# Image loads on ScalarE's queue, and small set-up steps moved between engines, in a two-layer table convolution

## The chip, the core and the metric

The kernel runs on one core of a Trainium2 chip. A core has four engines that compute: TensorE (matrix products, "PE" in the profile, with its weight loads as "PEld"), VectorE ("DVE"), ScalarE ("ACT") and GpSimd ("POOL"). Each works through its own list of instructions in order and waits for the others by semaphores. SyncE ("SP") only begins transfers here. Transfers between the chip's memory (DRAM) and the core's on-chip memory (SBUF) are done by 16 DMA engines; TensorE writes into a small memory of its own (PSUM), which VectorE and ScalarE read. The metric is the device time of one execution in microseconds (us), the lower the better.

## What is computed

The input x holds 16 images of 256 channels, 28 x 28. It is normalised in groups of 8 channels (`_gn`), and goes through two convolutions that are computed by tables: each channel's 3 x 3 patch is compared with 16 centroids, a softmax over the 16 turns the distances into weights, and the weights pick from a table that holds each centroid's product with the convolution's weights.

```python
def amm_conv3x3(x, centroids, w_sub, stride=1):
    ...
    d = jnp.sum(p * p, axis=-1)[..., None] - 2.0 * jnp.einsum('bncs,cks->bnck', p, centroids) + jnp.sum(centroids * centroids, axis=-1)[None, None]
    attn = jax.nn.softmax(-d, axis=-1)
    lut = jnp.einsum('cks,cso->cko', centroids, w_sub)
    out = jnp.einsum('bnck,cko->bno', attn, lut)
...
out = amm_conv3x3(x, centroids1, wsub1, stride=1)
out = jax.nn.relu(bn_inference(out, bn1_gamma, bn1_beta, bn1_mean, bn1_var))
out = amm_conv3x3(out, centroids2, wsub2, stride=1)
out = bn_inference(out, bn2_gamma, bn2_beta, bn2_mean, bn2_var)
out = se_layer(out, se_w1, se_b1, se_w2, se_b2)
return jax.nn.relu(out + x)
...
x = x + _L0_conv_ref(_gn(x), ...)
```

`bn_inference` scales and shifts each channel with given statistics; `se_layer` scales each channel by a gate worked out from the channels' means.

## The kernel before

**Blocks and steps.** The first layer is done for all 16 images, then the second. An image is cut into four blocks: two halves of 128 channels (hh) by two halves of 14 rows (t), 392 positions each, in the order (0,0), (0,1), (1,1), (1,0). A block takes two steps, an image eight; step 8b is the first of image b in the first layer.

**A block's work.** For a block the 3 x 3 patches lie in two buffers, `pts[0]` and `pts[1]`, one for each half of the 128 channels' groups. The products of patches and centroids, the logits (`logits`, L609), are computed by 32 x 32 tiles in four groups, each into two PSUM banks of a pair; ScalarE takes their exponentials (`exps`, L620). With these, `num_b` (L674, "nb") gives the sums of the softmax's denominators, which are taken apart by `split_r` (L684) and `split_q` (L694) on ScalarE and `join_r` (L688) and `join_q` (L699) on VectorE and inverted by `recip_dve` (L702); `spread` (L713, L717) copies the inverses across partitions. `num_a` (L660, "na") sums the weights of the 16 centroids into nine codes; they are scaled by the inverses either by VectorE straight from PSUM (`scale_a`, L736) or copied by ScalarE (`copy_a`, L730) and scaled by GpSimd (`scale_q`, L725). Then come the table products with 128 x 128 tiles (`product`, L744), for which GpSimd first makes differences of two blocks' codes (`mix`, L753): by a scheme like Strassen's, an image's 2 x 2 blocks need seven products in place of eight. `acc_copy`, `acc_add`, `reg_add` and `norm_out` put the results together.

**Order.** The order is written out by hand. `at(step, sub, f, ...)` files a job under a pair of numbers; at the end all jobs are run through in the order of the pairs, and each puts its instructions at the end of its engine's list. Two jobs with different pairs stand in that order on every engine that both use, and in every DMA queue. PSUM is handed out in four tags of two banks each (0 to 3, "bank" and "banks" in the code); for the first image a table gives the tags. A job that writes a bank waits until the one before has been read.

**Images.** Images of the first layer are loaded whole (`load_x`, L186, into `xt`), normalised (`gn_stats`, `gn_mean` L530, `gn_var`, `gn_apply`) and written into a padded copy in DRAM, `home`; a block's patches are read from there by six transfers (`patches`, at step g + p - 2, sub 1.5, p = 0 or 1), all begun by SP. `load_x(b + 1)` stands at step 8b - 2, sub 2.6, and so behind a step's six patch transfers in SP's queue. In the second layer `load_x` brings the image for the last sum.

**The first image.** No patches of a normalised image exist yet at the start. So the first image's patches are taken from the raw x, loaded straight into `pts` and into `alts` (the buffers of the table, "wall" in the profile, which are filled with 1.0 first, since patches at the rim have places that no transfer writes), and the normalisation is put into the centroids: each centroid weight is scaled by the group's inverse deviation, and shifted in such a way that the mean falls out. The steps for one half of the channels, each once for either half h of the nine taps' weights:

- `raw_stats`, `raw_mean`, `raw_dev`, `raw_root`: statistics of the groups, up to a power of -0.5 on GpSimd (L473), the "root";
- `sq_act`, `sq_sum` (L374), `sq_add`: the sum of squares of the centroids;
- `mean_off`: subtracts the mean over the 16 centroids from the weights (a reduction and an add);
- `raw_scales`: spreads the root to 16 columns (L477, VectorE), brings them by a product with `eighth` (L478, "gnq") to all partitions and makes from it the scales `scm` (L481) and shifts `ms`;
- `tap_sum` (L390): a product that sums the weights of a tap, `tap_scale` (L397): weights times scale, `tap_shift` (L405 multiplies the tap's sum by the shift into `tmp`, L408 adds it);
- `border` (L512, L515, and GpSimd's L512, L520, L525): adds the mean's terms at the rim of the patches.

```python
def tap_shift(hh, h):
    tmp = rpool.tile([P, N], F32, tag="r", name="tmp")[:, :256].rearrange("p (g n) -> p g n", n=32)
    ...
    nc.vector.tensor_tensor(
        tmp, raws.pop(("tap", hh, h)).rearrange("p (g n) -> p g n", n=32), of16(raws["ms", hh], h), ALU.mult
    )
    nc.vector.tensor_tensor(w, w, tmp, ALU.add)
```

These steps come for channel half 0 before the first logits (the steps of h = 1 partly between them), and for channel half 1 within the first steps (`later`, step 1, sub 0.9; `later_tap` and `tap_shift` at step 3). ScalarE fills `alts[1]` and GpSimd `alts[0]` (L1487). `setup_bn` (step 6, sub 2.75) makes the scales and shifts of both layers' `norm_out`: four steps on GpSimd (L311, L312) and VectorE's small steps behind them (L326 among them), in one function. Image 1 is normalised within step 4: `gn_mean` at 0.81, `gn_var` at 0.83, `acc_copy` at 0.85, the shuffles that `scale_a` of block 1 needs at 0.815 and 0.835.

A flag that is summed at the end decides whether a loop behind the main program computes everything a second time in a safer way; for these inputs it is not entered.

## Time and profile before

| | |
|---|---|
| median of 3 runs | 2611.18 us (2610.99 to 2613.4) |
| the profiled execution, its own time | 2614.36 us |
| its span in the trace | 2612.9 us |
| TensorE's products (PE) / weight loads (PEld) | 99% / 49% of the span |
| VectorE / ScalarE / GpSimd | 68% / 52% / 73% |
| the DMA queue that SP and ScalarE use | 48% of 16 engines' span |
| read from DRAM / written | 288.46 MB / 77.95 MB |

How to read the rows below. A row of groups or waits names the engine, the operation, the tile written and the tiles read ("out<-in") and the line of the kernel; a row of the timeline begins with the start and the duration in us from the start of the span, then the engine, the line and the shape, "xN" instructions taken together, and in brackets the idle time of the engine just before with the work that ended it ("issue" where the profile shows none). A row of waits ends in the sum of the waits in us, their number, and the longest. A row of stretches gives the stretch, its length, then the busy time of TensorE, weight loads, VectorE, ScalarE and GpSimd with the number of instructions, the granted clock of TensorE, the DMA engines' busy share, and GB/s. "SPq" is the start of a transfer from SP's queue.

### The profile page before, as it was taken

Reading aid. Unit: us, or ns where it says so; the run is one execution under the profiler, and the core shown is the slowest. Engines: PE = TensorE matmul, PEld = TensorE weight load, DVE = VectorE, ACT = ScalarE, POOL = GpSimd, SP = SyncE. Lnnn points to the kernel's source line nnn. Section 1 sums busy time; section 2 is a strip of 40 time slices with the busy share of each in tenths; the row PEclk is TensorE's granted clock in tenths of the full one; section 3 lists DMA queues with packets and bytes.
Section 4 is the critical chain, followed back from the end, with each engine's and each line's share of the span. In section 5 each row is a group of like instructions: output and inputs, shape, how many; then the busy total and the mean of one; then the engine's idle time right before and its main releaser. Section 6 shows DMA issues by size and latency. Waiting matters only on the chain.

```text
span 2612.9 us, 85829 instructions
## 1 busy us (share of the span) xinstructions
PE 2590.2 (99%) x37026; PEld 1273.7 (49%) x37026; DVE 1779.5 (68%) x3798; ACT 1369.3 (52%) x1912; POOL 1908.8 (73%) x1341
## 2 busy tenths in 40 slices
PE   8999999999999999999999999999999999999998
PEld 3444454444444444444444444444444444444444
DVE  8776656666566665566666776767776667767676
ACT  5444444444444454444454655555555655555565
POOL 6786666866568766676666787778878788787786
PEclk9999999999999999999999999999999999999999
DMA  6556656665555566655664444444444444444442
GB/s 212 152 150 183 201 155 186 165 170 165 159 143 144 170 182 179 170 154 141 176 172 107 106 118 119 126 115 117 104 130 123 120 117 110 115 126 127 117 104 66
DMA packets 213288, 372.07 MB, mean 142 GB/s; under 512 B 29496, under 2 KB 183528, under 8 KB 212328
## 3 DMA queue, kind: packets, MB, share of 16 engines
q1 hardware_dynamic: 206584, 333.75, 48.0%
q0 software_dynamic: 6176, 32.66, 3.5%
q8 instruction: 295, 4.83, 0.8%
q14 instruction: 89, 0.73, 0.1%
q10 hardware_dynamic: 144, 0.10, 0.0%
HBM read 288.46 MB, written 77.95 MB: 140 GB/s over the span
## 4 chain that ended last, share of the span: by engine, by line
PE 97%; DVE 1%; POOL 1%; issue 0%; ACT 0%; DMA 0%; SPq 0%; ACTq 0%; POOLq 0%
PE acc L744 52%; PE lg L609 17%; PE nb L674 14%; PE na L660 14%; POOL qp L753 0%; DVE rb L717 0%; DVE r L702 0%; PE sep L1045 0%; ACT e L620 0%; PE sep L1037 0%; DMA xt<-in_x 0%; DVE gn_st L424 0%; DVE qp L736 0%; DVE first L477 0%; PE tap L390 0%
## 5 line engine op out<-in xcount | busy, mean ns | idle before, releaser
L744 PE MATMUL acc<-qp,wall 128*128 128x392 f32 (+1 forms) x3088 | 1097.7, 498 | 0.3 <-POOL qp L753 0.2
L620 ACT ACTIVATE e<-lg 128x784 f32<-128x784 f32 x960 | 738.2, 820 | 642.9 <-PE lg L609 639.7
L753 POOL TENSOR_TENSOR qp<-qp,qp 128x784 f32<-128x784 f32 x512 | 945.0, 1870 | 153.3 <-DVE qp L736 152.9
L744 PEld LDWEIGHTS acc<-qp,wall 128*128 128x128 f32 x3088 | 568.5, 190 | 503.9 <-issue 53.0
L717 DVE STREAM_SHUFFLE rb<-r 128x392 f32<-128x392 f32 x1024 | 551.1, 605 | 0.0
L609 PE MATMUL lg<-pt,wd 32*32 32x392 f32 x15872 | 470.1, 499 | 1.0 <-DMA pt<-home 0.4
L688 DVE SCALAR_TENSOR_TENSOR r<-nb,kst,r 128x392 f32<-128x392 f32 x128 | 80.0, 625 | 445.1 <-ACT r L684 444.4
L674 PE MATMUL nb<-e,cwb 64*32 64x392 f32 x8192 | 374.1, 492 | 0.4 <-ACT e L620 0.3
L660 PE MATMUL na<-e,cwa 64*32 64x392 f32 x8192 | 374.3, 492 | 0.0
L736 DVE TENSOR_TENSOR qp<-na,rb 128x784 f32<-128x784 f32 x352 | 333.7, 972 | 59.1 <-PE na L660 47.3
L725 POOL TENSOR_TENSOR qo<-qo,rb 128x392 f32<-128x392 f32 x128 | 131.3, 1026 | 299.3 <-DVE rb L713 298.6
L702 DVE RECIPROCAL r<-r 128x392 f32<-128x392 f32 x128 | 333.2, 2603 | 4.4
L725 POOL TENSOR_TENSOR qp<-qp,rb 128x784 f32<-128x784 f32 x160 | 295.9, 1860 | 3.0
L674 PEld LDWEIGHTS nb<-e,cwb 64*32 64x32 f32 x8192 | 190.9, 107 | 174.2 <-issue 23.8
L660 PEld LDWEIGHTS na<-e,cwa 64*32 64x32 f32 x8192 | 183.0, 106 | 182.2 <-issue 73.8
L609 PEld LDWEIGHTS lg<-pt,wd 32*32 32x32 f32 x15872 | 116.7, 103 | 268.4 <-issue 241.0
L744 PE MATMUL acc<-qp,w_A 128*128 128x392 f32 x512 | 182.7, 499 | 0.0
L684 ACT ACTIVATE r<-nb,kst 128x392 f32<-128x392 f32 x128 | 86.7, 677 | 166.4 <-PE nb L674 163.3
L644 POOL TENSOR_TENSOR z<-z,mx 128x1568 f32<-128x1568 f32 x32 | 91.8, 2869 | 94.8 <-DVE mx L638 94.8
L744 PE MATMUL acc<-qo,wall 128*128 128x392 f32 (+1 forms) x386 | 157.9, 491 | 0.0
L730 ACT COPY qp<-na 128x784 f32<-128x784 f32 x160 | 130.0, 813 | 22.0 <-PE na L660 20.5
L744 PEld LDWEIGHTS acc<-qp,w_A 128*128 128x128 f32 x512 | 94.7, 190 | 82.1 <-DVE qp L736 19.8
(242 smaller groups left out, 1713.3 us busy)
## 6 DMA issues: line engine op xcount, KB each, us to landing
pt<-home SPq DMA_DIRECT2D x744, 209.0 KB
pt<-home SPq DMA_DIRECT2D x744, 104.5 KB
home<-xpad SPq DMA_DIRECT2D x30, 899.0 KB
xt<-in_x SPq DMA_DIRECT2D x30, 784.0 KB
out_dram<-y SPq DMA_DIRECT2D x31, 392.0 KB
pt<-in_p SPq DMA_DIRECT2D x6, 784.0 KB
d_wS<-st SPq DMA_DIRECT2D x12, 192.0 KB
wall<-d_wS SPq DMA_DIRECT2D x4, 576.0 KB
```

Source lines behind the costliest of these rows:

```text
L609: nc.tensor.matmul(bk[32 * c : 32 * c + 32, :N].rearrange("p (r w) -> p r w", w=W), lhsT=(wx[u["hh"]] if early(u) else wts["wd", u["hh"]]) ...
L620: nc.scalar.activation(eg[:, 2 * i : 2 * i + 2, :], bk[:, :, :N], AF.Exp, scale=2.0)
L644: nc.gpsimd.tensor_tensor(zk, zk, mx.unsqueeze(2).to_broadcast([P, N // 4, K]), ALU.subtract)
L660: nc.tensor.matmul(bs[32 * i : 32 * i + 32, r, :N], lhsT=wts["cwa", u["hh"]][64 * r : 64 * r + 64, mm, i, :], rhs=es[64 * r : 64 * r + 64, ...
L674: nc.tensor.matmul(bs[32 * i : 32 * i + 32, r, :N], lhsT=wts["cwb", u["hh"]][64 * r : 64 * r + 64, mm, i, :], rhs=es[64 * r : 64 * r + 64, ...
L702: nc.vector.reciprocal(u["r"], u["r"])
L717: nc.vector.stream_shuffle(rb[:, r, :], u["r"], mask_of(2 * mm + r))
L725: nc.gpsimd.tensor_tensor(q, q, u.pop(("rb", mm)), ALU.mult)
L730: nc.scalar.copy(pair(u, mm), u.pop(("na", mm))[:, :, :N])
L736: nc.vector.tensor_mul(pair(u, mm), u.pop(("na", mm))[:, :, :N], rb)
L744: nc.tensor.matmul(accs[key][:, : cols[1] - cols[0]], lhsT=wl[w][:, k, :], rhs=us["q", k][:, cols[0] : cols[1]], start=first and n == 0, s ...
L753: nc.gpsimd.tensor_tensor(pair(out_u, mm), pair(in0, mm), pair(in1, mm), ALU.subtract)
```

## The change

- `load_x` can be begun by another engine. The loads of images 2 to 15 in the first layer, b + 1 with b > 1 and thus 13 loads from image 3 on, are now begun by ScalarE at step 8b - 2, sub 0.12, right behind the first two exps of the step and ahead of the step's patches. Images 1 and 2 are loaded as before (image 2 at step 7, sub 1.6).
- The fill of `alts[0]` goes from GpSimd (L1487) to ScalarE, which now fills both.
- In `raw_scales` the scaling of 16 columns (L477) goes from VectorE to GpSimd.
- The second half's `mean_off` moves from between `raw_scales` and `tap_scale` of the first half to step -0.4, sub 0.5, behind the border of the first patches; the second half's `tap_scale` follows at 0.55.
- The second half's `tap_sum` moves to step 0, sub 0.15, between the first and the second group of logits, from tag 2 to tag 3; its `tap_shift` follows at step 0, sub 0.2.
- `tap_shift` multiplies in place, in PSUM, and the add reads its product from there; `tmp` is gone.
- For channel half 1 one small step of `raw_dev` becomes a function of its own, `raw_sum`, run within `mean_off` between the reduction and the add.
- `gn_mean` and `gn_var` of image 1 move within step 4 from 0.81 and 0.83 to 0.825 and 0.845, behind the shuffles at 0.815 and 0.835.
- `setup_bn` keeps the four steps on GpSimd; VectorE's seven small steps become `setup_shift`, at step 9, sub 2.1.

```diff
--- before.py
+++ after.py
@@ -178,12 +178,12 @@
         return pts[i].rearrange("p s n -> p (s n)")[:, n0 : n0 + n]
 
-    def load_x(b, spare=False):
+    def load_x(b, spare=False, eng=None):
         if spare:
             t = spare_of(0, NB * HW).rearrange("p (b n) -> p b n", b=NB)
         else:
             t = io.tile([P, NB, HW], F32, tag="xt", name="xt")
-        nc.sync.dma_start(t, x[b].rearrange("(b p) n -> p b n", p=P))
+        (eng or nc.sync).dma_start(t, x[b].rearrange("(b p) n -> p b n", p=P))
         xs[b] = t
@@ -317,16 +317,19 @@
 
     def setup_bn():
-        nc.vector.tensor_scalar_mul(nb2_sb, vecs[:, :, 8], -1.0)
         for l in range(2):
-            ga, be, mu, va = (vecs[:, :, 4 * l + i] for i in range(4))
             sc = const.tile([P, NB], F32, name=f"bnsc{l}")
             sh = const.tile([P, NB], F32, name=f"bnsh{l}")
-            rsqrt(sc, va, BN_EPS, NB)
+            rsqrt(sc, vecs[:, :, 4 * l + 3], BN_EPS, NB)
+            bn.append((sc, sh))
+
+    def setup_shift():
+        nc.vector.tensor_scalar_mul(nb2_sb, vecs[:, :, 8], -1.0)
+        for l, (sc, sh) in enumerate(bn):
+            ga, be, mu = (vecs[:, :, 4 * l + i] for i in range(3))
             nc.vector.tensor_mul(sc, sc, ga)
             nc.vector.tensor_mul(sh, mu, sc)
             nc.vector.tensor_sub(sh, be, sh)
-            bn.append((sc, sh))
 
@@ -378,10 +381,12 @@
         nc.vector.tensor_add(w, w, raws.pop(("sqp", hh, h)))
 
-    def mean_off(hh, c0, c1):
+    def mean_off(hh, c0, c1, mid=None):
         g = wflat(hh)[:, c0:c1].rearrange("p (g k) -> p g k", k=K)
         m = cst[:, c0 // K : c1 // K]
         nc.vector.tensor_reduce(m, g, axis=AX.X, op=ALU.add)
+        if mid:
+            mid()
         nc.vector.scalar_tensor_tensor(
@@ -400,12 +405,10 @@
 
     def tap_shift(hh, h):
-        tmp = rpool.tile([P, N], F32, tag="r", name="tmp")[:, :256].rearrange("p (g n) -> p g n", n=32)
         w = wx[hh].rearrange("p a b c -> p (a b) c")[:, 8 * h : 8 * h + 8]
-        nc.vector.tensor_tensor(
-            tmp, raws.pop(("tap", hh, h)).rearrange("p (g n) -> p g n", n=32), of16(raws["ms", hh], h), ALU.mult
-        )
-        nc.vector.tensor_tensor(w, w, tmp, ALU.add)
+        t = raws.pop(("tap", hh, h)).rearrange("p (g n) -> p g n", n=32)
+        nc.vector.tensor_tensor(t, t, of16(raws["ms", hh], h), ALU.mult)
+        nc.vector.tensor_tensor(w, t, w, ALU.add)
 
@@ -438,15 +441,17 @@
 
     def raw_dev(k):
-        ps, rr, mean = raws["ps", k], raws["rr", k], gst[0][1][:, k, 0:1]
+        ps, mean = raws["ps", k], gst[0][1][:, k, 0:1]
         dv = piece(2)
         nc.vector.tensor_sub(dv[:, 0:1], ps[:, 0:1], mean)
         nc.vector.scalar_tensor_tensor(dv[:, 1:2], ps[:, 0:1], mean, dv[:, 0:1], op0=ALU.subtract, op1=ALU.mult)
-        if k:
-            nc.vector.scalar_tensor_tensor(rr[:, 0], hot_sb[:, :16], dv[:, 1:2], rr[:, 2], op0=ALU.mult, op1=ALU.add)
         gm = piece(2)
         nc.vector.tensor_copy(gm, ps[:, :2])
         raws["dv", k], raws["gm", k] = dv, gm
+
+    def raw_sum(k):
+        rr, dv = raws["rr", k], raws["dv", k]
+        nc.vector.scalar_tensor_tensor(rr[:, 0], hot_sb[:, :16], dv[:, 1:2], rr[:, 2], op0=ALU.mult, op1=ALU.add)
 
@@ -474,7 +479,7 @@
     def raw_scales(ps):
         rr, rstd = raws["rr", 0], nrm[:, 0, 1, 0:1]
-        nc.vector.tensor_scalar(rr[:, 0], hot_sb[:, :16], rstd, None, op0=ALU.mult)
+        nc.gpsimd.tensor_scalar(rr[:, 0], hot_sb[:, :16], rstd, None, op0=ALU.mult)
         nc.tensor.matmul(ps[:, 16:32], lhsT=eighth, rhs=rr[:, 0], start=True, stop=True)
@@ -1380,11 +1385,14 @@
                             at(g + 12 + o + (o and r), (0.06, 1.97)[r] if o == 0 else (1.805, 2.9)[r], to_home2, b, o, r)
                 if b + 1 < B:
-                    at(*((g - 2 + (b == 1), 2.6 - (b == 1)) if b else (1, 1.6)), load_x, b + 1)
+                    if b > 1:
+                        at(g - 2, 0.12, load_x, b + 1, eng=nc.scalar)
+                    else:
+                        at(*((7, 1.6) if b else (1, 1.6)), load_x, b + 1)
                     for q in range(NB):
                         at(*(((g + 1, 1.5) if b == 1 else (g, 0.3)) if b else (3, 1.3)), gn_stats, b + 1, q)
-                    at(*((g + 1, 2.1) if b else (4, 0.81)), gn_mean, b + 1, step=g + 1 if b else 4)
-                    at(*((g + 3, 2.1) if b else (4, 0.83)), gn_var, b + 1, step=g + 3 if b else 4)
+                    at(*((g + 1, 2.1) if b else (4, 0.825)), gn_mean, b + 1, step=g + 1 if b else 4)
+                    at(*((g + 3, 2.1) if b else (4, 0.845)), gn_var, b + 1, step=g + 3 if b else 4)
                     for q in range(NB):
@@ -1477,25 +1485,25 @@
     sq_act(0, 0)
     sq_act(0, 1)
-    nc.scalar.activation(alts[1].rearrange("p s n -> p (s n)"), one.to_broadcast([P, 8 * PTW]), AF.Copy)
+    for t in alts:
+        nc.scalar.activation(t.rearrange("p s n -> p (s n)"), one.to_broadcast([P, 8 * PTW]), AF.Copy)
     raw_stats(0)
     raw_mean(0, bank("gnp", tag=0))
     raw_dev(0)
     sq_sum(0, 0, bank("sqp", tag=1)[:, :256])
     ps = bank("gnq", tag=3)
     raw_root(ps)
-    nc.gpsimd.memset(alts[0], 1.0)
     sq_sum(0, 1, bank("sqp", tag=2)[:, :256])
     raw_means(0)
     mean_off(0, 0, 256)
     raw_scales(ps)
     tap_sum(0, 0, bank("tap", tag=0)[:, :256])
-    mean_off(0, 256, 512)
-    tap_sum(0, 1, bank("tap", tag=2)[:, :256])
     tap_scale(0, 0)
     tap_shift(0, 0)
-    at(-0.4, 0.5, tap_scale, 0, 1)
-    at(-0.4, 0.6, tap_shift, 0, 1)
+    at(-0.4, 0.5, mean_off, 0, 256, 512)
+    at(-0.4, 0.55, tap_scale, 0, 1)
+    at(0, 0.15, lambda: tap_sum(0, 1, bank("tap", tag=3)[:, :256]))
+    at(0, 0.2, tap_shift, 0, 1)
     for t in xpads:
@@ -1509,7 +1517,7 @@
         for h in range(2):
             sq_add(1, h)
-        mean_off(1, 0, 512)
+        mean_off(1, 0, 512, lambda: raw_sum(1))
 
@@ -1529,6 +1537,7 @@
         at(3, 0.91, tap_shift, 1, h)
     at(6, 2.75, setup_bn)
+    at(9, 2.1, setup_shift)
     for t in hpads:
```

## The prediction

> **What bounds the kernel now.** I read the page first, then TensorE's waits, then the first 80 us engine by engine.
>
> ```profile
> span 2612.9 us, 85829 instructions
> PE 2590.2 (99%) x37026; PEld 1273.7 (49%) x37026; DVE 1779.5 (68%) x3798; ACT 1369.3 (52%) x1912; POOL 1908.8 (73%) x1341
> ```
>
> TensorE is busy for 2590.2 of 2612.9 us. The change leaves its work as it is (one small product moves), so all that can be won lies in 22.7 us of idle time, and more than 5 us needs most of what can be reached. The waits of TensorE, and two stretches, say where it is:
>
> ```profile
> PE lg L609 <- issue: 4.2, 3, 2.2
> PE gnq L478 <- DVE wd L379: 2.9, 1, 2.9
> PE gnp L530 <- DVE gn_mv L425: 0.3, 1, 0.3
> ...
> 60.00:80.00 20.00, 17.33 (x322) 7.32 (x304) 14.13 (x34) 9.79 (x15) 18.09 (x18) 1.00 0.58 173
> 80.00:100.00 20.00, 20.00 (x268) 10.41 (x254) 15.44 (x38) 7.80 (x11) 20.00 (x12) 1.00 0.81 205
> ...
> 400.00:1300.00 900.00, 898.71 (x12878) 441.47 (x12862) 574.68 (x1316) 423.54 (x581) 615.15 (x470) 1.00 0.59 164
> ```
>
> In a stretch's row the second figure is TensorE's busy time, the fifth GpSimd's. The 2.9 us and part of the 4.2 come before the first logits. Stretch 60 to 80 has 2.67 us of idle time (20.00 - 17.33), the long stretch of the first layer 1.29 us in 900. The second layer has none to give. So the sum has three places: the beginning, 60 to 80, and the loads.
>
> **The beginning.** What holds it is seen on VectorE, GpSimd and TensorE together:
>
> ```profile
> 8.85 2.89 POOL L1487 MEMSET wall<- 128x3360 f32 x1
> 14.46 1.09 POOL L512 TENSOR_TENSOR pt<-pt,first 128x208 f32<-128x208 f32 x1 [2.73 <-DVE tmp L405]
> ...
> 9.13 2.64 DVE L477 TENSOR_SCALAR first<-hot_sb,nrm 128x16 f32<-128x16 f32 x1
> 12.47 0.29 DVE L481 TENSOR_SCALAR first<-gnq,hot_sb 128x16 f32<-128x16 f32 x1 [0.70 <-PE gnq L478]
> 13.55 0.42 DVE L397 TENSOR_TENSOR first<-wd,first 128x256 f32<-128x256 f32 x1
> 14.68 1.27 DVE L512 TENSOR_TENSOR pt<-pt,first 128x224 f32<-128x224 f32 x1
> 15.99 0.49 DVE L515 SCALAR_TENSOR_TENSOR pt<-pt,hot_sb,first 128x224 f32<-128x224 f32 x1
> ...
> 11.82 0.61 PE L478 MATMUL gnq<-first,hpad 128*128 128x16 f32 x2 [2.92 <-DVE wd L379]
> 12.27 1.20 PE L390 MATMUL tap<-wd,nhalf_sb 128*128 128x256 f32 x2
> 16.58 6.27 PE L609 MATMUL lg<-pt,first 32*32 32x392 f32 x128 [1.67 <-issue]
> 24.39 2.87 PE L674 MATMUL nb<-e,cwb 64*32 64x392 f32 x64
> ```
>
> A scaling of 16 elements (L477) takes 2.64 us and ends at 11.77, with GpSimd's fill (8.85 + 2.89 = 11.74). It is no slow instruction: it stands until the fill is done. The same shows later, where VectorE adds two SBUF tensors while GpSimd multiplies:
>
> ```profile
> 37.95 3.88 POOL L725 TENSOR_TENSOR qp<-qp,rb 128x784 f32<-128x784 f32 x2
> 40.02 0.41 DVE L405 TENSOR_TENSOR tmp<-tap,first 128x256 f32<-128x256 f32 x1
> 40.46 1.65 DVE L408 TENSOR_TENSOR first<-first,tmp 128x256 f32<-128x256 f32 x1
> ```
>
> Such a step takes 0.42 us alone (L397 at 13.55) and, as L408, 1.65 us here; L405, which has one operand in PSUM, takes 0.41 in the same crowd. So an add that reads its product from PSUM is priced at 0.42 us. L512 at 14.68 fits too: it ends 0.4 us after GpSimd's first border step (14.46 + 1.09 = 15.55).
>
> After the change: the root is done when the fill now begins, at 8.85; the scaling on GpSimd has a row of its size, 0.35 us:
>
> ```profile
> 31.26 0.35 POOL L493 TENSOR_SCALAR first<-first,hot_sb 128x16 f32<-128x16 f32 x1
> ```
>
> so L478 starts at 9.3 (not 11.82) and VectorE has its result 0.65 us later (11.82 to 12.47), at 9.95. The second half's mean (what lies between 12.47 + 0.29 = 12.76 and 13.55, 0.79 us) moves behind the border. The tap product then runs 9.75 to 10.95 and sets the pace: shift's product at 11.0, its add at 11.45, border at 11.8. GpSimd's border waits for its images until 14.46, so this time the two borders don't meet: about 0.45 + 0.45 us instead of 1.80, and the first logits at 12.9 (bounds: 12.8, and 13.7 if the border stays at 1.80). That is 3.7 us sooner than 16.58 (2.9 to 3.8). The fill goes to ScalarE, which is free from 18.23 - 9.19 = 9.04 (row below); at GpSimd's 2.9 us it is done by 12.0, before any exp. Its cover gone, it would cost those 2.9 us.
>
> Part of it is given back before nb (24.39, 7.81 us after the first logits):
>
> ```profile
> 18.23 6.12 ACT L620 ACTIVATE e<-lg 128x784 f32<-128x784 f32 x8 [9.19 <-PE lg L609]
> ```
>
> ScalarE's eight exps set the pace there, starting 1.65 us behind the logits. Now a tap product (1.2 us) stands between the first and the second group of logits, in PSUM bank 3, which the second group also needs. A group takes about 1.3 us (an estimate, under the 6.27 / 4 = 1.57 that it takes with its waits). The bank comes free when both shift steps are done: 1.3 + 1.2 + 2 x 0.42 and two handovers, 3.4 us after the first logits. Only then can the rest of the second group start, and its exps near 4.45 us, while ScalarE is free at 1.65 + 2 x 6.12 / 8 = 3.18. So the exps lose 1.25 us (0.2 if the half in bank 2 goes ahead alone, 1.8 if the tap product waits for the late mean).
>
> The array's speed takes a second share:
>
> ```profile
> 6.42 1.20 PE L374 MATMUL sqp<-sq,nhalf_sb 128*128 128x256 f32 x2
> 22.88 0.38 PE L436 MATMUL sqp<-gn_mv,gmat 128*128 128x2 f32 x2
> 23.34 1.11 PE L374 MATMUL sqp<-sq,nhalf_sb 128*128 128x256 f32 x4
> ```
>
> Two passes took 1.20 us early, four took 1.11 us at 23.34; the granted clock, 1.00 in all the stretches above, does not show it. If TensorE comes to the small products of the second channel half before it is fast, these, which now take 24.39 - 22.88 = 1.5 us with 0.4 for small ones ahead, cost about 1.3 us more, since each pass takes twice the time: I charge half of it, 0.65 (0 to 1.3). The Trainium skill (TensorE: Matmul & The Clock Gate, Part 1) says the array runs at half clock until a free-running window of about 3.4 us was busy; that speaks against this change, since an earlier start does not move the window. The trace agrees as far as the two rows go. By that rule the whole 1.3 is charged and the forecast below is 0.65 us later, 2607.65.
>
> Beginning: 3.7 - 1.25 - 0.65 = **1.8 us** (bounds 2.9 - 1.8 - 1.3 = -0.2 and 3.8 - 0.2 = 3.6).
>
> **60 to 80.** The 2.19 us are these:
>
> ```profile
> 69.21 0.16 DVE L326 TENSOR_TENSOR bnsc<-bnsc,vecs 128x2 f32<-128x2 f32 x1 [1.81 <-POOL bnsc L312]
> 70.69 2.73 DVE L736 TENSOR_TENSOR qp<-na,rb 128x784 f32<-128x784 f32 x3
> 71.75 0.95 PE L609 MATMUL lg<-pt,first 32*32 32x392 f32 x32 [2.19 <-issue]
> ```
>
> VectorE waits for GpSimd's roots in setup_bn, so it scales na only from 70.69, and the logits wait for that PSUM bank (the first of three products ends at 70.69 + 0.91 = 71.6). With setup_shift at step 9 VectorE goes on at 69.21 - 1.81 = 67.4 and the wait is gone. Next late is GpSimd, busy for all of 80 to 100:
>
> ```profile
> 52.11 0.25 POOL L311 TENSOR_SCALAR rs_t<-gn_var 128x2 f32<-128x2 f32 x1
> 54.67 6.65 POOL L753 TENSOR_TENSOR qp<-qp,qp 128x784 f32<-128x784 f32 x3 [0.91 <-DVE qp L736]
> 71.73 6.65 POOL L753 TENSOR_TENSOR qp<-qp,qp 128x784 f32<-128x784 f32 x3 [1.55 <-DVE qp L736]
> 92.96 1.86 POOL L753 TENSOR_TENSOR qp<-qp,qp 128x784 f32<-128x784 f32 x1
> 95.78 1.48 PE L744 MATMUL acc<-qp,wall 128*128 128x392 f32 x4
> ```
>
> The mix that ends at 94.82 is read at 95.78: 0.96 us of slack. GpSimd's own 1.55 us wait at 71.73 goes, but gn_var now stands on VectorE behind six more shuffles, right ahead of the first scaling of na, which by the mix at 54.67 that waits for it began at about 54.67 - 0.95 = 53.7. So GpSimd's four steps for gn_var (52.11 to 54.67 - 0.91 = 53.76, 1.65 us) begin near 53.75, end near 55.4, and push all up to 71.73 - 1.55 = 70.18 by 0.75. GpSimd gains 1.55 - 0.75 = 0.8, TensorE 0.8 + 0.96, say **1.7 us** (0.8 to 2.2). gn_mean's 0.3 us wait goes, but gn_apply then comes later in front of an exp: counted 0 (-0.4 to 0.3). setup_shift's seven small steps (some 1.5 us) lie in this idle time, 2.89 us:
>
> ```profile
> 101.86 0.63 DVE L688 SCALAR_TENSOR_TENSOR r<-nb,kst,r 128x392 f32<-128x392 f32 x1 [2.89 <-ACT r L684]
> ```
>
> Without that cover they would cost up to 0.5. raw_sum, moved by one reduction, stays within nb.
>
> **The loads.** Thirteen leave SP's queue, where each stood behind six patch transfers, for ScalarE's:
>
> ```profile
> 463.00:466.00 3.00, 3.00 (x74) 1.33 (x59) 0.64 (x3) 1.50 (x3) 3.00 (x3) 1.00 0.00 0
> 630.73 0.39 SPq L186 DMA_DIRECT2D xt<-in_x  x1
> 464.61 0.68 ACT L684 ACTIVATE r<-nb,kst 128x392 f32<-128x392 f32 x1 [1.31 <-PE nb L674]
> 638.02 0.95 PE L609 MATMUL lg<-pt,wd 32*32 32x392 f32 x32 [0.36 <-DMA pt<-home]
> ```
>
> The new place is right behind two exps, in this stretch at 464.61 - 1.31 = 463.3: ScalarE idles 1.31 us there, which covers an issue of 0.39, and the transfer engines stand still (0.00). Behind the issue on ScalarE wait split_r, two exps and split_q, and for these VectorE and TensorE; nothing else. What it can win: 0.36 us at 638, where patches landed late 7 us after the load at 630.73, and one like it among the "issue" waits: **0.7 us** (0 to 0.9). VectorE's waits for the images cost TensorE nothing today.
>
> **Sum.** 1.8 + 1.7 + 0.7 = 4.2 us off the profiled execution's own time, 2614.36 (span 2612.9 and 1.46 around it): 2610.2. That execution lies 3.18 above the median 2611.18, so the median should come to **2607.0**. Its own range is 2605.0 to 2609.5.
>
> **Rivals.** 0.2% is 5.2 us, about what a measurement of this kernel can tell from no change.
> - All three terms near their upper ends: no cold products and little given back (2.9), 2.2, 0.9 and 0.3 make 6.3 us, 2604.9. For it: GpSimd's wait at 71.73 may move more than I count. Against: it is busy 18.09 of 20 us there. Chance 0.22.
> - The first images bind, so the scaling was not what held the logits. For it: GpSimd's border waited to 14.46, most likely for its images. Against: VectorE's images are issued before those. The border would start at 14.5, logits at 15.5, 1.1 sooner less 1.25: nothing is left there. 4.2 - 1.8 = 2.4, 2608.8. Chance 0.10.
> - Slower: ScalarE is held at the load, because a DMA's issue waits until an earlier transfer of the same semaphore has landed. From 1.31 - 0.39 = 0.92 us of wait on, each further us holds split_r and with it reciprocal and logits. At 1 us for each of 13 loads 13 - 4.2 = 8.8 us slower, 2620. Against: the row at 463 shows no transfer under way. The Trainium skill (DMA: Bandwidth & Descriptors, Queues, rings and completion order) adds that the engines take turns between queues packet by packet, so a load on ScalarE's queue would share with a patch set rather than stand behind it; the same row has nothing to share with. Chance 0.07.
>
> **How the numbers follow.** The forecast keeps 0.61. Faster by over 0.2% (below 2606.0): 0.22 and a small tail of the forecast, 0.25. Slower: 0.07. Within: 0.68. The range, 2604.0 to 2611.0, leaves out the third rival and the ends of the first.
>
> **What would show it.** First logits near 12.9, with no long small step on VectorE before; nb between 22 and 23.5; no 2 us wait near 70, but short waits for GpSimd's mixes between 80 and 96; no wait for patches near 638; ScalarE's load issue short, with split_r behind it on time. I am wrong if the first logits come after 14, if nb comes after 24, or if exps wait behind a load.

## The result, and the profile after

The changed kernel takes 2620.15 us in the median (2617.91 to 2624.99, 7 runs) against 2612.35 us before (2610.99 to 2613.4, 7 runs): a ratio of 1.0034, 95% interval 1.0024 to 1.0044. It is 7.8 us slower in the medians, where 4.2 us faster was forecast. The two profiled executions lie above these medians, by 2.0 us before (2614.36) and by 2.3 after (2622.49). One execution of a run below (setup_shift behind the acc_adds) took 3740 us at a granted clock of 0.66 and is left out of that run's median. First the page's head, then TensorE's waits:

```profile
span 2621.0 us, 85833 instructions
PE 2593.9 (99%) x37026; PEld 1272.4 (49%) x37026; DVE 1777.7 (68%) x3797; ACT 1371.9 (52%) x1913; POOL 1905.6 (73%) x1341
...
PE lg L614 <- DMA pt<-home: 7.8, 2, 4.9
...
PE lg L614 <- issue: 2.0, 1, 2.0
PE lg L614 <- DVE hpad L786: 2.0, 1, 2.0
PE na L665 <- DVE gn_var L562: 1.4, 1, 1.4
```

The wait of 2.19 us near 70 is gone, and so are the 2.9 us before the product with `eighth` (0.6 are left). The wait put down to "issue" lies before the first logits. New are two waits for patches, 7.8 us together, one of 2.0 us for an `acc_add` (L786), and one of 1.4 us for `gn_var`. TensorE's busy time has also grown, by 3.7 us, with the same 37026 products: some of them ran slower.

Where the time went is read by setting the two executions side by side, each group of products at its start in the timelines:

| start of | before, us | after, us | after - before |
|---|---|---|---|
| first logits | 16.58 | 13.01 | -3.57 |
| nb of block 0 | 24.39 | 24.32 | -0.07 |
| na of block 1 | 52.61 | 54.02 | +1.41 |
| nb of block 3 | 76.63 | 75.50 | -1.13 |
| na of block 4 | 108.89 | 109.98 | +1.09 |
| na of block 7 | 167.37 | 174.29 | +6.92 |
| nb of block 39 | 802.65 | 805.96 | +3.31 |
| na of block 47 | 973.93 | 983.54 | +9.61 |
| na of the last block | 2577.29 | 2585.65 | +8.36 |

So the beginning's lead is gone by the first nb, the stretch 60 to 80 wins 2.5 us, the stretch to 109 loses 2.2, two places near 160 and 964 lose 5.8 and over 6 us, and the rest of the first layer wins back 4.9 (6.92 - 3.31 and 9.61 - 8.36).

**The two waits for patches.** The timelines of ScalarE's and SP's queues, TensorE's timeline, and stretches around the first wait (the clock is the figure behind GpSimd's busy time, then the transfer engines' share):

```profile
139.57 2.37 SPq L863 DMA_DIRECT2D d_sc<-score_t  x2
142.59 0.43 ACTq L186 DMA_DIRECT2D xt<-in_x  x1
147.04 0.33 SPq L866 DMA_DIRECT2D d_h<-hpad  x1
...
950.85 0.40 ACTq L186 DMA_DIRECT2D xt<-in_x  x1
948.57 11.80 SPq L592 DMA_DIRECT2D pt<-home  x5
959.77 2.50 SPq L592 DMA_DIRECT2D pt<-home  x4
...
159.84 1.62 PE L614 MATMUL lg<-pt,wd 32*32 32x392 f32 x32 [2.90 <-DMA pt<-home]
963.99 1.62 PE L614 MATMUL lg<-pt,wd 32*32 32x392 f32 x32 [4.89 <-DMA pt<-home]
...
158.00:161.00 3.00, 1.16 (x32) 0.32 (x32) 1.56 (x6) 0.00 (x0) 2.92 (x4) 0.67 0.91 196
161.00:164.00 3.00, 3.00 (x48) 1.02 (x40) 1.53 (x5) 1.54 (x2) 3.00 (x3) 0.50 0.32 94
164.00:167.00 3.00, 3.00 (x72) 1.06 (x56) 0.00 (x0) 0.46 (x1) 3.00 (x3) 0.70 0.03 5
...
959.05:964.00 4.95, 0.06 (x3) 0.04 (x3) 1.84 (x7) 0.49 (x1) 0.00 (x0) 0.71 0.54 160
```

SP begins four transfers of a patch set between 948.57 and 951.9 and then stands; the fifth begins at 959.77. The last packet of ScalarE's load (begun at 950.85) ends at 959.05. Near 142 it is the same with another transfer: `d_h` begins at 147.04, and the last packet of the load of 142.59 ends at 146.65. SP waits for the load to land although nothing that it moves has to do with that image. The built program's list of instructions says why. Each row has its place in its engine's list and, in brackets, the semaphores that it waits for; DMAHW6 is number 6 below (the first row is ScalarE's, the others SP's):

```
625 L186 DMACopy xt_11035<-in_x 128x2x784 [waits DMAHW6_49,Activation_49]
...
620 L250 DMACopy w1_sb_145<-in_se_w1 128x2x16 [waits DMAHW5_49]
621 L251 DMACopy w2_sb_146<-in_se_w2 16x128 [waits DMAHW7_49]
...
628 L592 DMACopy pt1_69<-home1_11_90 8x8x418 [waits DMAHW6_49]
```

SP's and ScalarE's transfers take turns at eight semaphores, and one that takes a semaphore waits until the last transfer that had it has landed. The turn is fixed when the program is built. Number 6 falls to the load, between two small transfers (5 and 7) that SP begins long before it, and then to the fifth of the patch set (row 628). SP, kept by the small transfers (938.62 to 945.11) and by one that it begins at 948.12, begins this set only 2.3 us before the load, and so the load is in the air when the fifth is due; at the load before (870.82) SP was done with the same set at 867.6. For the load of 142.59 the number is 3, and the next transfer with number 3 is the `d_h` of 147.04.

The logits that wait for the set start 2.90 and 4.89 us late, and behind the wait TensorE runs at half its clock (0.50), so that 32 logits take 1.62 us and not 0.94. Near 160 the half clock lasts from 158.99 to 165.82. What of it lies behind the wait, 165.82 - 159.84 = 5.98 us, costs half of itself: 2.90 + 2.99 = 5.89 us, where the table's rows between block 4 and block 7 show 6.92 - 1.09 = 5.83.

**The beginning.** TensorE's timeline of the changed kernel, and that of the run with the loads back on SP, in which the beginning is the same program:

```profile
13.01 1.62 PE L614 MATMUL lg<-pt,first 32*32 32x392 f32 x32 [1.97 <-issue]
22.33 2.05 PE L377 MATMUL sqp<-sq,nhalf_sb 128*128 128x256 f32 x4
24.32 3.60 PE L679 MATMUL nb<-e,cwb 64*32 64x392 f32 x64
...
21.35 1.11 PE L377 MATMUL sqp<-sq,nhalf_sb 128*128 128x256 f32 x4
22.39 2.87 PE L679 MATMUL nb<-e,cwb 64*32 64x392 f32 x64
```

The first logits start where they were forecast. In the first execution the four sqp passes take 2.05 us, so the array is still slow at 24.3; in the second 1.11, and nb starts 2.0 us earlier than before the change. Which of the two comes differs between executions, though the beginning is the same: of ten profiled executions with it, nb starts at 22.3 to 22.6 us in seven, and at 24.3 to 24.4 in three.

**gn_var and setup_shift.** VectorE, GpSimd and TensorE of the changed kernel, and the stretch 60 to 80; the last row is the two `acc_add`s in the kernel before:

```profile
53.82 0.15 DVE L562 TENSOR_TENSOR gn_var<-gn_gm,gnp 128x2 f32<-128x2 f32 x1
54.02 2.21 PE L665 MATMUL na<-e,cwa 64*32 64x392 f32 x48 [1.36 <-DVE gn_var L562]
...
96.99 3.10 DVE L327 TENSOR_SCALAR nb_sb<-vecs 128x2 f32<-128x2 f32 x1
98.19 1.88 POOL L730 TENSOR_TENSOR qp<-qp,rb 128x784 f32<-128x784 f32 x1
100.92 1.03 DVE L786 TENSOR_TENSOR hpad<-acc,hpad 128x392 f32<-128x392 f32 x2
102.11 0.95 PE L614 MATMUL lg<-pt,wd 32*32 32x392 f32 x32 [1.95 <-DVE hpad L786]
...
60.00:80.00 20.00, 19.80 (x361) 8.33 (x342) 15.58 (x31) 11.35 (x16) 19.64 (x18) 1.00 0.70 202
...
97.94 1.03 DVE L781 TENSOR_TENSOR hpad<-acc,hpad 128x392 f32<-128x392 f32 x2
```

`setup_shift`'s first step works on 2 columns and stands for 3.10 us, until GpSimd's L730 ends (98.19 + 1.88 = 100.07). Only behind its seven steps come the two `acc_add`s, at 100.92 and not at 97.94, and they free the PSUM bank that the logits of 102.11 wait for. The Trainium skill (SBUF — State Buffer, SBUF: two separate sides) says that VectorE and GpSimd share a pair of ports as a lock, held for a whole instruction, when a VectorE step runs in a two-port mode, or reads two SBUF tensors beside a GpSimd step that reads SBUF. The trace agrees: the six steps behind this one, of the same size, take 0.15 or 0.16 us each, and this one ends with GpSimd's.

### The profile page after: what moved, and what is told of

Its sections match the earlier page's. It is cut to its first block, busy times and chain, and to the rows that moved or that the text cites. A ratio compares the mean times of both kernels' runs of the same rounds, so it can differ in the third digit from the quotient of the medians.

```text
span 2621.0 us, 85833 instructions
## 1 busy us (share of the span) xinstructions
PE 2593.9 (99%) x37026; PEld 1272.4 (49%) x37026; DVE 1777.7 (68%) x3797; ACT 1371.9 (52%) x1913; POOL 1905.6 (73%) x1341
## 4 chain that ended last, share of the span: by engine, by line
PE 97%; DVE 1%; DMA 1%; POOL 0%; ACT 0%; issue 0%; SPq 0%; POOLq 0%; ACTq 0%
PE acc L749 52%; PE lg L614 17%; PE na L665 14%; PE nb L679 14%; DMA xt<-in_x 0%; DVE rb L722 0%; PE sep L1050 0%; DMA pt<-home 0%; ACT e L625 0%; POOL qp L758 0%; SPq L592 0%; PE tap L395 0%; PE sep L1042 0%; DVE nb_sb L327 0%; PE sqp L377 0%
## 5 line engine op out<-in xcount | busy, mean ns | idle before, releaser
L730 POOL TENSOR_TENSOR qo<-qo,rb 128x392 f32<-128x392 f32 x128 | 131.3, 1026 | 290.7 <-DVE rb L718 289.9
L730 POOL TENSOR_TENSOR qp<-qp,rb 128x784 f32<-128x784 f32 x160 | 295.5, 1857 | 3.0
```

Of the source, the lines that this page charges most:

```text
L730: nc.gpsimd.tensor_tensor(q, q, u.pop(("rb", mm)), ALU.mult)
```

## The experiments

Each ran beside the kernel before on the same chip; the ratios are to that kernel, whose median lay between 2612.4 and 2613.6 us. Most intervals are 0.0009 either way, 2.4 us, so where two runs differ by one or two us, it is the traces that show it and not the medians. Five start from the changed kernel with two loads put back, called "two loads back" below.

**Loads back on SP.** All else of the change stays.

```diff
-                    if b > 1:
-                        at(g - 2, 0.12, load_x, b + 1, eng=nc.scalar)
-                    else:
-                        at(*((7, 1.6) if b else (1, 1.6)), load_x, b + 1)
+                    at(*((g - 2 + (b == 1), 2.6 - (b == 1)) if b else (1, 1.6)), load_x, b + 1)
```

> The changed kernel, but with all thirteen loads on SP's queue at their old place. Theory (the loads lose two waits of 5.8 and 6.8 us and win some 4.5 us elsewhere; all else in the change adds up to +1.1 us): 2613.4 us, 1.1 above the kernel before; no wait of TensorE for patches over 1 us; the late first steps stay (nb first at 24.3 us, a wait of 2 us near 102). Rival (the rest of the change is worth the 3.5 us that was forecast for it, and the trace of the changed kernel misled): 2608.9 us.

Measured: 2610.7 us, ratio 0.9992 (0.9983 to 1.0002). No wait for patches; the waits of 2.0 us at 101 and 1.3 us at 53 are there. It lies between the two forecasts. nb started at 22.39, 2 us earlier than in the execution from which the +1.1 was read, but half clock near 43 (last section) took 1.7 us of that back: by na of block 4 TensorE is 0.16 us behind the kernel before. From block 7 to the end of the first layer it then wins 3.0 us, with no load on ScalarE. So most of the 4.9 us above is not the loads' doing; that the kernel before's profiled execution was 2.0 us above its median is likely a part of it. All that the change does beside the loads is worth 1.7 us in the medians, not clear of nothing, and the loads make the loss.

**Only the loads.** The kernel before with the thirteen loads on ScalarE, the diff above the other way round.

> The kernel before, with the thirteen loads on ScalarE's queue and nothing else of the change. Theory (the loads alone cost 5.8 + 6.8 us and win about 4.5 elsewhere): some 7.5 us above the kernel before, 2619 to 2621 us, with both waits for patches near 160 and 964. Rival (the waits come from the loads together with the other moves, which shift ScalarE's and SP's times against each other): 2608 to 2612 us.

Measured: 2621.87 us, ratio 1.0035 (1.0023 to 1.0046). One wait is listed under patches, that near 964; SP's `d_h` again begins right behind the load's landing (last packet at 146.53):

```profile
PE lg L609 <- DMA pt<-home: 4.4, 1, 4.4
...
142.44 0.42 ACTq L186 DMA_DIRECT2D xt<-in_x  x1
146.92 0.33 SPq L861 DMA_DIRECT2D d_h<-hpad  x1
```

The place near 160 loses 6.4 us here (from block 6 to block 7), in a wait of 1.6 us of the logits, which the profile puts down to a VectorE step, in two of 1.9 and 0.9 us of the products behind them for GpSimd, and in 3.4 us at half clock. So the loads alone cost the whole of it, 9.5 us, a little more than was expected, without any other part.

**Two loads back.** Only the loads of images 3 and 13 return to SP.

```diff
-                    if b > 1:
+                    if b > 1 and b not in (2, 12):
...
-                        at(*((7, 1.6) if b else (1, 1.6)), load_x, b + 1)
+                        at(*((g - 2 + (b == 1), 2.6 - (b == 1)) if b else (1, 1.6)), load_x, b + 1)
```

> The changed kernel, with the loads of images 3 and 13 alone back on SP's queue; the other eleven stay with ScalarE. Theory (a patch transfer of SP's queue waits for the semaphore that one of these two loads still holds): both waits near 160 and 964 go with their slow clock after, 2620.15 - 5.83 - 6.75 = 2607.6 us. Rival (any load on a second queue can make the patches late, where it falls is chance): waits of the same size come at other loads, 2614 to 2620 us.

Measured: 2610.09 us, ratio 0.9990 (0.9981 to 1.0000). Both waits are gone and none came elsewhere but 0.6 us at 317. The median is 2.5 us above the 2607.6 of the theory, which took its prices from an execution 2.3 us above the changed kernel's median; the two profiled spans, 2621.0 and 2608.8, lie 12.2 us apart, where 12.6 was expected. Eleven loads on ScalarE do no harm that shows; against the run with all on SP they win 0.6 us in the medians and 1.0 in the spans, near what was forecast for all thirteen, but less than the runs can tell apart.

**Another queue.** The loads are begun by GpSimd at the new place.

```diff
-                        at(g - 2, 0.12, load_x, b + 1, eng=nc.scalar)
+                        at(g - 2, 0.12, load_x, b + 1, eng=nc.gpsimd)
```

> The changed kernel, with the thirteen loads begun by GpSimd at the same place in the order, on a queue that has its own semaphores. Theory (the shared semaphore is what holds SP's patches, not the shared transfer engines): no wait of TensorE for patches over 1 us near 160 and 964, 2607 to 2610 us, unless GpSimd itself is late, which its mixes would show. Rival (two queues at once share the transfer engines, and the patches come late for that): both waits stay, 2618 to 2622 us.

Measured: 2626.38 us, ratio 1.0048 (1.0031 to 1.0065), slower than both forecasts. The wait near 160 is gone, but ten of 0.8 to 2.6 us stand behind other loads (near 236, 317, 400, 564 and on, and one of 2.3 us near 972). The profile puts three of them down to patches and most others to VectorE's steps just before. Behind the load begun at 307.68 only 8 to 70 KB of patches move per us between 311 and 316, while GpSimd's queue, with the load and two copies into `home`, moves 180 to 310 KB. So sharing the transfer engines can make patches late too, and this run does not settle what the semaphore does.

**The same semaphore elsewhere.** SP's six small transfers, which make it late at step 92, are filed at step 84.

```diff
-    at(92, 2.3, load_se)
+    at(84, 2.3, load_se)
```

> The changed kernel, with SP's six small transfers of the gate's weights filed at step 84 and not at step 92, so that they stand ahead of image 12's load and no longer of image 13's; nothing else. Theory (a wait comes where SP is kept busy before a load, for then a patch transfer that is given the load's semaphore next is still to be begun when the load is): the wait of 4.9 us at 964 goes and one like it comes at image 12's load, some 80 us earlier, and the time stays at 2617 to 2623 us. Rival (image 13's load is late for another reason): the wait stays near 964, none near 883.

Measured: 2617.87 us, ratio 1.0020 (1.0011 to 1.0029). The wait at 964 is gone and one has come at image 12's load:

```profile
877.30 1.25 SPq L592 DMA_DIRECT2D pt<-home  x2
...
880.94 0.95 PE L614 MATMUL lg<-pt,wd 32*32 32x392 f32 x32 [1.40 <-DMA pt<-home]
```

The sixth transfer of a set, due at 870.6, begins at 877.30; the last packet of the load of 871.29 ends at 876.79. The place follows SP's lateness, as the theory says, though this wait is 1.4 and not 4.9 us: one transfer is held here, not two.

**Two small transfers ahead of image 13's load.** They hand the semaphores on by two places and leave the load as it is.

```diff
+    tiny_sb = const.tile([1, 8], F32, name="tiny_sb")
+
+    def tiny(n):
+        nc.scalar.dma_start(tiny_sb[:, 4 * n : 4 * n + 4], x[0, 0:1, 4 * n : 4 * n + 4])
...
+                        for n in range(2 if b == 12 else 0):
+                            at(g - 2, 0.12, tiny, n)
                         at(g - 2, 0.12, load_x, b + 1, eng=nc.scalar)
```

> The changed kernel, with two transfers of 16 bytes begun by ScalarE just ahead of image 13's load, so that the eight semaphores are handed on by two places: in the list of instructions the transfer that needs the semaphore of this load next is then the first of the following patch set, and no longer the fifth of the set that SP is about to begin; the two small ones come before the third and the fifth. The load, its queue, its time and all that it shares with the patches stay. Theory (what holds the patches at 964 is the semaphore): that wait of 4.9 us falls below 2 us, the one of 2.9 us near 160 stays, 2613 to 2616 us. Rival (the patches are late because SP was kept busy and two queues share the transfer engines): the wait near 964 stays at 4 to 5 us, 2618 to 2622 us.

Measured: 2618.64 us, ratio 1.0022 (1.0012 to 1.0031), 5.5 us above the kernel before where the changed kernel was 7.8. The time lies in the rival's range, the wait between the two.

```profile
956.17 2.61 SPq L597 DMA_DIRECT2D pt<-home  x4
...
963.72 0.99 PE L619 MATMUL lg<-pt,wd 32*32 32x392 f32 x32 [2.87 <-DMA pt<-home]
```

SP goes on at 956.17, 4 us ahead of the load's last packet (960.29), where it stood until 0.7 us behind it in the changed kernel: it no longer waits for the load. It waits for the small transfer now, begun at 952.55, and that alone takes 3.6 us. So the hold is the semaphore's. But the wait falls by 2.0 us and not by 3 or more: from the end of the sixth transfer's issue to the logits it takes 4.9 us (958.78 to 963.72) and in the changed kernel 3.0 (961.00 to 963.99). That these patches were slower because they shared the transfer engines with the load is likely, and not shown; the rival would then be right on that part of the wait.

**The new place on SP's queue.** All thirteen loads on SP, at step 8b - 2, sub 0.12.

```diff
-                        at(g - 2, 0.12, load_x, b + 1, eng=nc.scalar)
+                        at(g - 2, 0.12, load_x, b + 1)
```

> The changed kernel, with all thirteen loads at their new place in the order, ahead of the step's patches, but on SP's queue. Theory (the place in the order is what lets patches land in time; the second queue only adds that a semaphore is held over SP's transfers): no wait for patches near 160 or 964, and none near 557 and 638, 2609 to 2610.5 us. Rival (the second queue is needed for the gain, since on SP's the load stands in front of the patches): the load makes the patches behind it late, 2612 us or more.

Measured: 2614.57 us, ratio 1.0004 (0.9995 to 1.0013), as the rival said. The small waits near 557 and 638 are gone, but ahead of the patches in one queue the load holds them where SP is late (3.88 us):

```profile
946.59 0.39 SPq L186 DMA_DIRECT2D xt<-in_x  x1
...
963.45 1.62 PE L614 MATMUL lg<-pt,wd 32*32 32x392 f32 x32 [3.88 <-DMA pt<-home]
```

**setup_shift behind the acc_adds.** From "two loads back".

```diff
-    at(9, 2.1, setup_shift)
+    at(10, 0.07, setup_shift)
```

> The kernel with the loads of images 3 and 13 back on SP (2610.1 us), and setup_shift's seven steps behind the two acc_adds of step 10 and not ahead of them. Theory (setup_shift's first step stands 3.1 us until GpSimd's running step ends, and the acc_add behind it frees the logits' PSUM bank): the wait of 1.7 to 2.0 us at 102 goes, 2608.1 us, with the first logits of that step near 100. Rival (the held step now delays join_r, which has only 2.9 us of idle time before it): half of the gain is lost, 2609.1 us.

Measured: 2612.17 us (ten executions), ratio 0.9999 (0.9989 to 1.0008): 2.1 us more than "two loads back", where 2 less was expected. The wait at 102 is gone and a longer one has come at 110:

```profile
97.34 3.09 DVE L327 TENSOR_SCALAR nb_sb<-vecs 128x2 f32<-128x2 f32 x1
...
101.48 1.77 DVE L332 TENSOR_TENSOR bnsh<-vecs,bnsh 128x2 f32<-128x2 f32 x1
...
105.09 1.76 DVE L332 TENSOR_TENSOR bnsh<-vecs,bnsh 128x2 f32<-128x2 f32 x1
106.77 0.61 DVE L693 SCALAR_TENSOR_TENSOR r<-nb,kst,r 128x392 f32<-128x392 f32 x1
...
110.58 0.95 PE L614 MATMUL lg<-pt,wd 32*32 32x392 f32 x32 [4.03 <-issue]
```

Here GpSimd's steps follow one another without a gap, and four of the other six steps are held as well: seven steps fill 97.34 to 106.85, 9.5 us, and `join_r` begins at 106.77, where it began at 101.86 before the change. The mechanism was right, the price far too low.

**setup_shift on GpSimd.** From "two loads back", behind the mixes of step 10.

```diff
-        nc.vector.tensor_scalar_mul(nb2_sb, vecs[:, :, 8], -1.0)
+        nc.gpsimd.tensor_scalar(nb2_sb, vecs[:, :, 8], -1.0, None, op0=ALU.mult)
...
-            nc.vector.tensor_mul(sc, sc, ga)
-            nc.vector.tensor_mul(sh, mu, sc)
-            nc.vector.tensor_sub(sh, be, sh)
+            nc.gpsimd.tensor_tensor(sc, sc, ga, ALU.mult)
+            nc.gpsimd.tensor_tensor(sh, mu, sc, ALU.mult)
+            nc.gpsimd.tensor_tensor(sh, be, sh, ALU.subtract)
...
-    at(9, 2.1, setup_shift)
+    at(10, 2.6, setup_shift)
```

> The kernel with the loads of images 3 and 13 back on SP (2610.1 us), and setup_shift's seven steps done by GpSimd, behind its mixes of step 10, where it waits 2.9 us for the next shuffle. Theory (VectorE's small steps on two SBUF operands stand still while GpSimd computes, so they must not be on VectorE there at all): the wait near 102 goes, none comes near 110, 2608.1 us. Rival (GpSimd is what binds in this stretch, so its seven more steps, some 1.5 us, come back as waits for its mixes): 2609.6 us or more.

Measured: 2608.71 us, ratio 0.9983 (0.9974 to 0.9992), 4.9 us below its kernel before, where "two loads back" is 2.3 below. Neither wait is left; the steps take 0.2 us each in GpSimd's idle time:

```profile
110.42 0.24 POOL L327 TENSOR_SCALAR nb_sb<-vecs 128x2 f32<-128x2 f32 x1
...
111.85 0.19 POOL L332 TENSOR_TENSOR bnsh<-vecs,bnsh 128x2 f32<-128x2 f32 x1
```

**gn_mean and gn_var back.** From "two loads back".

```diff
-                    at(*((g + 1, 2.1) if b else (4, 0.825)), gn_mean, b + 1, step=g + 1 if b else 4)
-                    at(*((g + 3, 2.1) if b else (4, 0.845)), gn_var, b + 1, step=g + 3 if b else 4)
+                    at(*((g + 1, 2.1) if b else (4, 0.81)), gn_mean, b + 1, step=g + 1 if b else 4)
+                    at(*((g + 3, 2.1) if b else (4, 0.83)), gn_var, b + 1, step=g + 3 if b else 4)
```

> The kernel with the loads of images 3 and 13 back on SP (2610.1 us), and gn_mean and gn_var of image 1 at their old place, ahead of the shuffles. Theory (gn_var behind six shuffles holds a PSUM bank, and the na product waits 1.34 us for it): that wait goes and the old one of 0.31 us is back, 2609.2 us. Rival (the later place is what let VectorE's shuffles and GpSimd's mixes go early, and its gain is in the stretch 60 to 80): the wait goes, but TensorE is not ahead at 75 us, 2610 to 2611 us.

Measured: 2608.97 us, ratio 0.9986 (0.9977 to 0.9995), as the theory said. The wait for `gn_var` is gone, 0.31 us is back, and between na of block 1 and nb of block 3 TensorE still wins 2.56 us (2.54 in the changed kernel), so that gain does not come from `gn_var`'s place; the split of `setup_bn` is what is left for it.

**Products on zeros.** From "two loads back": four before the first small products, two before the first logits; their results are not read.

```diff
+    half_sum = const.tile([P, N], F32, name="half_sum")
+    nc.vector.memset(half_sum, 0.0)
...
-    half_sum = const.tile([P, N], F32, name="half_sum")
...
+    def warm(n, tag):
+        ps = bank("hot_ps", tag=tag)
+        for _ in range(n):
+            nc.tensor.matmul(ps[:, :N], lhsT=half_sum[:, :P], rhs=half_sum, start=True, stop=True)
+
+    warm(4, 3)
     sq_act(0, 0)
...
+    warm(2, 2)
     tap_scale(0, 0)
```

> The kernel with the loads of images 3 and 13 back on SP (2610.1 us), with four products of 392 columns on zeros before the first small products and two more before the first logits, whose results nothing reads. Theory (the array is at half speed in the first 20 to 26 us for want of work before, and it is this that eats part of the earlier start): the products of 392 columns take 0.49 us from the first logits on, nb first begins near 21 and not 22.3 us, 2608.5 us, and single executions spread less. Rival (ScalarE's exps set the pace there, so a fast array wins nothing): nb first at 22 or later, 2610 us.

Measured: 2608.47 us, ratio 0.9983 (0.9974 to 0.9992), nb first at 21.28, and executions from 2605.94 to 2609.35 where "two loads back" has 2608.25 to 2613.86. The first four products take 5.6 us and hold the first statistics up by 1.5 us (7.01 and not 5.49), so this is not yet the best number of them.

**All of it.** Two loads back, gn back, setup_shift on GpSimd, products on zeros.

> The same as the run before, and beside it gn_mean and gn_var at their old place and the products on zeros that keep the array busy. Theory (the four findings are independent): 2610.1 - 2.0 (setup_shift) - 1.1 (gn) - 1.6 (array) = 2605.4 us, with no wait of TensorE over 1 us after 20 us. Rival (an earlier TensorE runs into the next late thing, GpSimd's mixes or the patches): 2607 to 2608.5 us.

Measured: 2606.88 us (2604.61 to 2609.44), ratio 0.9976 (0.9967 to 0.9985): 0.24% faster than the kernel before and faster than every other. Against the kernel before of the same runs that is 6.7 us; 2605.4 would have been 7.0 below the 2612.4 that the expectation started from. Taken from the runs one by one, each against its own kernel before, the parts make 8.0 (2.3 for "two loads back", and 2.6, 1.3 and 1.8 more for the other three), so they add up but for 1.3 us, which the runs can't tell from nothing. In this execution the array is fast from the first logits on, and after 20 us TensorE has no wait over 1.0 us:

```profile
11.86 0.95 PE L615 MATMUL lg<-pt,first 32*32 32x392 f32 x32 [0.80 <-PE hot_ps L1491]
...
19.88 2.86 PE L680 MATMUL nb<-e,cwb 64*32 64x392 f32 x64
```

## Why the prediction was wrong

- **The loads, 0.7 us won.** This is the step that failed. The gain is about what eleven loads measure (0.6 to 1.0 us), though the runs can't tell that from nothing. What was missed is the cost, about 12 us at two of them (5.8 near 160, 6.3 near 964). The prediction asked what is queued behind the load on ScalarE and found "nothing else" than `split_r` and what follows. It did not ask which of SP's transfers gets the load's semaphore next. The third rival had the mechanism, an issue that waits until an earlier transfer of the same semaphore has landed, but held ScalarE with it; that it gave nearly the time (2620) is luck, 13 times 1 us in place of twice 6. ScalarE was not held: in the changed kernel `split_r` follows the load of 142.59 at 145.21, behind 1.31 us of idle time, as in the prediction's row. SP was, at 2 of 13 loads for 5 and 8 us, not at all of them for 1 us. The row quoted against it, with no transfer under way, came from a stretch where SP is on time.
- **The beginning, 1.8 us.** First logits at 13.01, forecast 12.9: every step up to there held, with no held step on VectorE. nb starts 1.8 to 2.1 us earlier in seven of ten executions, as forecast, and not at all in three. The array's share was charged at 0.65 us as a mean; it is 0 or 2, by the execution, so the mean of the ten is near that and no single execution is. In four of the seven, half clock near 43 then takes 1.7 us back, which the prediction does not have.
- **60 to 80, 1.7 us.** It won 2.54, above the range given (2.2). GpSimd did not hold it back by the 0.75 us charged for `gn_var`: with `gn_var` early or late the gain is the same within 0.02 us.
- **setup_shift, counted at nothing, 0.5 at most.** It cost 2.03 us (from nb to na of block 4). The rule that a VectorE step on SBUF operands stands until GpSimd's step is done was read correctly from L477 and L408, used for the scaling, and not applied to seven steps of the same kind in a stretch where GpSimd was known to be busy throughout. The `acc_add`s behind them in the order were not named either.
- **gn_mean and gn_var, counted at nothing (-0.4 to 0.3).** They cost 0.74 us in the changed kernel's execution, and put back they win 1.1 in the medians: what is late next is not an exp, but the na products, which wait for a PSUM bank that `gn_var` reads behind six shuffles.
- **The tap product in PSUM, raw_sum, the fill on ScalarE** cost nothing that shows: the fill ends at 11.84 us, the first exp starts at 14.66.

Without the two late loads the change measures 2.3 us faster (0.9990, interval up to 1.0000), against 4.2 forecast; setup_shift and gn_var, 2.8 us together, are more than the difference. The forecast of 2607.0 also stood on a median of three runs, 1.2 us under that of seven.

## What to carry to other kernels

Before a transfer is moved to another queue, list the completion semaphores in the order in which they are handed out: a transfer that lands late holds whatever comes next on its semaphore, above all where the other queue already runs late. A small VectorE step on SBUF operands costs what is left of GpSimd's running step, and several cost that several times, so beside a busy GpSimd they belong on GpSimd itself. A wait of TensorE is priced with what follows it, which may run at half clock.

## What was not expected of the hardware

An idle time of TensorE need not be long to cost its clock. In the run with the loads back on SP, 0.96 us of idle time at 41 was followed by half clock:

```profile
40.00:43.20 3.20, 2.24 (x39) 0.78 (x33) 2.67 (x4) 3.00 (x5) 2.79 (x5) 0.99 0.00 1
43.20:46.60 3.40, 3.40 (x7) 1.83 (x6) 3.33 (x9) 0.46 (x1) 0.00 (x0) 0.50 0.69 240
46.60:50.00 3.40, 3.40 (x13) 2.01 (x13) 1.47 (x9) 0.00 (x0) 1.63 (x3) 1.00 0.06 26
```

It lasted 3.41 us, so it cost 1.7, almost twice the idle time. The same 0.96 us stands in the changed kernel at 44 and in the kernel before at 43.77, with no such fall in their profiled executions. Near 160 and 964 it lasted 6.83 us, twice 3.41. In the changed kernel the clock changes at 25.87, 158.99, 165.82, 961.13 and 967.95 us, and each distance is a whole number of 3.413 us (39, 2, 233, 2). Cut into such pieces up to 2600 us, the fourteen profiled executions show more than the length of a gap does: every piece at full clock with 2.03 us of idle time or more (ten of them) was followed by half clock; of those with 0.95 to 1.96 us seven were, and most were not. The Trainium skill (TensorE: Matmul & The Clock Gate, HAM oscillation — how this bites in real kernels) gives a rule of no idle gaps over about 3.4 us. The runs agree with the length of the window, and not with that threshold: here 0.96 us was enough in some executions, and 2.03 us in all. That is also a likely part of the spread between runs of one kernel, but no run here was made to show it.
